# A decoder layer on one core: rules for when side work may be given out, row-tile due times, and the number of gather buffers

## The chip, the cores and the metric

The kernel runs on one core of a Trainium2 chip. The core has a matrix engine (TensorE, "PE" in the profile; its weight loads are listed apart as "PEld"), a vector engine (VectorE, "DVE"), a scalar engine (ScalarE, "ACT"), a general engine (GpSimd, "POOL"), and an engine that only issues transfers here (SyncE, "SP"). Each works through its own instructions in order; they wait for one another by semaphores. Transfers are carried by 16 DMA engines. TensorE writes into PSUM, a small memory of eight banks; everything else lies in SBUF or in the chip's main memory.

The metric is the device time of one execution, in microseconds; the median of the runs counts. A profiled execution gives the trace, which is told in microseconds from the start of its span.

## What is computed

A layer over 4 sequences of 512 tokens, 512 channels each, all in float32:

```python
x = x + attn(layernorm(x), wq, wk, wv, wo)      # 32 heads, 8 kv heads, width 64, rope, causal
x = x + xattn(layernorm(x), ctx)                # both sides rounded to fp8 per block, then a product
x = x + moe(layernorm(x), Wg, W1, W3, W2, sw1, sw3, sw2)

def quant_dequant_act_1x128(x):                 # weights: the same with one scale per 128x128 block
    xb = x.reshape(E, M, K // 128, 128)
    amax = jnp.max(jnp.abs(xb), axis=-1, keepdims=True)
    safe = jnp.maximum(amax, 1e-4)
    q = (xb * (448.0 / safe)).astype(jnp.float8_e4m3fn)
    return (q.astype(jnp.float32) * (safe / 448.0)).reshape(E, M, K)

# moe: each token goes to its best of 8 experts, at most 256 tokens an expert
out = jnp.take(oe, jnp.minimum(flat, E * C - 1), axis=0) * (gate * keep)[:, None]
shared = jax.nn.silu(xt @ sw1) * (xt @ sw3) @ sw2
return out + shared
```

The second term is no attention: each of the 4 sequences is multiplied with its own 512 x 512 context matrix after both were rounded block by block. The third has a shared feed-forward network for every token and eight routed ones.

## The kernel before, in words

The program is straight-line: Python code decides once in which order the instructions of every engine stand. Three stages follow one another.

**Attention with side work.** The scores of one batch are worked in 40 half steps (`SPB`), two to a step. In the loop at the end of the attention part (around L1122), a half step emits: the score matmuls of the next half step (`scores`, whose results VectorE takes to `pm` with the row minimum and ScalarE turns into exponentials), the products with v of finished heads (`weighted`), then fill work (`work.upto`), then the transposes of the probabilities (`turned`: `pt`, copied to `pT` half by ScalarE, half by VectorE, L981 and L987). The fill work is everything else: the projections q, k, v, o of this and the next batch, and the "chain" of the layers between: `CHAIN` at L719 names its jobs.

- `hs`, `h`: layer norm and transposes of the next batch's input (`job_h` L289: four transposes, each copied by ScalarE).
- `cs`, `c`: scales of the context matrix (`job_cs` L474: block maxima, a transpose `pam`, VectorE's `cmx` and `cdg` L493 and L495, a small product `par`) and its rounded, transposed form (`job_c` L503).
- `s`: row statistics after attention. `t`: one job for each of four row tiles (`job_t` L554): scale on GpSimd, round, transpose, four products `py` whose scaled results `y` (VectorE, L592, two buffers) are added to the rows by GpSimd.
- `w`: router, gates, positions, and the scatter of the rows to the experts' places.

A rounding (`quantize_round` L434) is four VectorE instructions on 128x512 elements, L438 to L445.

**The plan.** `Fill` keeps a book: `at` is its own clock, `spent` the TensorE work given out, `gpsimd` (L267 to L269) the moment up to which it believes GpSimd busy, `cool` a moment before which no further chain block is given out. A job is a Python generator. It yields a positive number for TensorE work done, a negative one for a pause in half steps, or a triple: a kind ("dve" or "quiet"), a pause, and how many microseconds of VectorE work come next. Such heavy pieces are given out against the half step's allowance (3.2 at L1122, 4.4 at L1128); a "quiet" one is passed over while `gpsimd` lies ahead of `at`. `first` (L809) picks the next job in order of wanted time, `step` (L827) runs it to its next yield and sets `cool` 0.2 half steps (a half step is `HALF`, 7250 ns) after each chain block, and `upto` (L847) alternates heavy pieces, chain blocks and projections until the half step's share is spent. `need` (L872) forces what the scores cannot wait for. PSUM's banks are shared by tag at L95: four "sp" (scores, `pt`), one "av", three "mm" for all fill work.

The due time of `t` job j is `ze + 2 + j`, counted in half steps (L795); jobs 2 and 3 also wait for jobs 0 and 1, j - 2 each.

**Shared expert and experts.** After the last scores the shared network's units (`shared_up`, `shared_down`) are TensorE's work, with what is left of the chain put in between every few matmuls (`between`, L1247). Then the eight experts run, each with its weights loaded ahead.

**The end.** The last units of the shared network run with rounds of up to four gathers: `gather` (L1328) asks for a row tile `xt` (six buffers, a load on SP's queue) and issues an indirect transfer of the experts' rows to `og` (five buffers, on GpSimd's queue); `combine` (L1338) adds them on VectorE and, where the row is finished, issues its store on SP's queue.

## Time and profile before

| | us |
|---|---|
| median of 3 runs | 1621.65 (1620.45 to 1622.72) |
| the profiled execution, its own time | 1620.97 |
| its span, from first to last instruction | 1619.2 |
| TensorE busy | 1569.1 |
| VectorE busy | 821.8 |
| ScalarE busy | 513.1 |
| GpSimd busy | 332.4 |
| mean granted TensorE clock | 0.989 of full |

How to read the profile's lines. A waits line names the engine, line and tile that waited, what ended the wait, and then total, number and longest. A timeline line gives start, length, engine, line, operation, tiles (written <- read), shapes and count; in brackets the engine's idle time before it and who ended that. A line of stretches gives the stretch, its length, each engine's busy time with its instructions, then the granted TensorE clock (PEclk), the busy share of the DMA engines, and GB/s. Ends of matmuls are modelled.

By stage, TensorE's busy time:

| stretch, us | length | PE busy | DVE busy | ACT busy | POOL busy |
|---|---|---|---|---|---|
| 0 to 80 | 80 | 76.10 | 35.44 | 29.45 | 13.11 |
| 80 to 440 | 360 | 351.29 | 224.44 | 152.75 | 80.03 |
| 440 to 800 | 360 | 340.31 | 235.26 | 146.27 | 103.19 |
| 800 to 1160 | 360 | 351.33 | 209.97 | 138.42 | 91.93 |
| 1160 to 1260 | 100 | 100.00 | 52.27 | 7.61 | 24.22 |
| 1260 to 1619 | 359 | 350.04 | 64.42 | 38.66 | 19.92 |

Attention with its side work ends a little before 1160; the shared network with the last batch's chain follows to about 1260, then the experts and the end.

### The profile page before, as it was taken

To read this page: it belongs to the slowest core of one execution; us is meant where nothing else is said; L and a number is where in the kernel's file an instruction comes from. 1 tells how busy PE (TensorE), PEld (TensorE's weight loads), DVE (VectorE), ACT (ScalarE), POOL (GpSimd) and SP (SyncE) were. 2 spreads that over 40 slices of the span, in tenths; PEclk is the share of its full clock that TensorE was granted. 3 is DMA by queue.
4 is the path that set the end of the run, shared out by engine and by line. 5 is a ranking of instruction groups with operands and counts; after the bars stand their busy time and mean duration, and the time that the engine had idled before them with its cause. 6 is when DMAs were issued, how large, how long until landed. Compare 5 with 4: busy or idle time off the path is not lost.

```text
span 1619.2 us, 19846 instructions
## 1 busy us (share of the span) xinstructions
PE 1569.1 (97%) x6664; PEld 861.4 (53%) x6664; DVE 821.8 (51%) x2399; ACT 513.1 (32%) x1539; POOL 332.4 (21%) x293
## 2 busy tenths in 40 slices
PE   9999999998999999998999999989999999999997
PEld 5555555554545545454555545455444557767653
DVE  4466644578865446885654587683355211111113
ACT  2445343443425343443434345351000101101100
POOL 2031220213342121325212033420232000000012
PEclk9999999999999999999999999999999999999999
DMA  4483441623435243443415251355141253556327
GB/s 137 119 241 98 94 129 46 163 78 87 106 90 138 69 120 112 98 99 91 133 48 159 73 135 36 93 167 177 45 170 39 65 201 131 169 165 234 133 84 254
DMA packets 118918, 195.32 MB, mean 121 GB/s; under 512 B 17184, under 2 KB 36640, under 8 KB 118304
## 3 DMA queue, kind: packets, MB, share of 16 engines
q10 hardware_dynamic: 65760, 101.46, 22.5%
q1 hardware_dynamic: 50496, 84.20, 16.9%
q0 software_dynamic: 2560, 8.39, 1.6%
q8 instruction: 53, 0.87, 0.2%
q14 instruction: 49, 0.40, 0.1%
HBM read 136.07 MB, written 28.57 MB: 102 GB/s over the span
## 4 chain that ended last, share of the span: by engine, by line
PE 82%; DVE 8%; DMA 4%; issue 1%; POOL 1%; ACT 1%; SPq 1%; ACTq 0%; DVEq 0%; POOLq 0%
PE py L397 14%; PE psq L303 11%; PE p_e L1162 9%; PE p_s L1162 9%; PE sc L920 8%; PE av L1001 7%; PE pt L970 6%; PE epy L1190 4%; PE psv L345 4%; PE ys L1190 3%; PE psk L303 3%; DVE pm L943 2%; DMA tsq<-t2q 1%; DMA xt<-x 1%; PE ptr_h L252 1%
## 5 line engine op out<-in xcount | busy, mean ns | idle before, releaser
L953 ACT ACTIVATE pm<-pm,mn 128x256 f32<-128x256 f32 (+3 forms) x512 | 281.0, 550 | 383.1 <-DVE mn L943 358.2
L943 DVE CUSTOM_DVE_ANT_0 pm<-sc,mask 128x256 f32<-128x256 f32 (+3 forms) x512 | 216.6, 486 | 100.3 <-PE sc L920 98.1
L303 PE MATMUL psq<-hT,wq 128*128 128x512 f32 x512 | 242.2, 609 | 7.7 <-DVE cmx L493 7.4
L397 PE MATMUL py<-wo,aT 128*128 128x512 f32 x512 | 242.1, 608 | 5.2 <-DVE y L592 4.8
L920 PE MATMUL sc<-kT,t1q 64*128 64x384 f32 (+3 forms) x1024 | 170.9, 450 | 12.4 <-DVE pT L987 7.5
L987 DVE COPY pT<-pt 128x128 f32<-128x128 f32 (+3 forms) x256 | 113.8, 484 | 118.3 <-PE pt L970 105.1
L268 POOL TENSOR_TENSOR t1q<-t1q,tsq 128x512 f32<-128x512 f32 x64 | 82.2, 1286 | 433.5 <-DMA tsq<-t2q 320.8
L970 PEld LDWEIGHTS pt<-ident,pm 128*128 128x128 f32 x1280 | 146.8, 142 | 36.0 <-issue 31.0
L970 PE MATMUL pt<-ident,pm 128*128 128x128 f32 x1280 | 155.6, 276 | 0.7 <-ACT pm L953 0.7
L1162 PE MATMUL p_s<-h3x,slot_s 128*128 128x512 f32 x352 | 155.6, 594 | 0.0
L1162 PE MATMUL p_e<-xT,slot_e 128*128 128x256 f32 x704 | 155.1, 380 | 0.0
L981 ACT COPY pT<-pt 128x128 f32<-128x128 f32 (+3 forms) x256 | 97.5, 431 | 180.3 <-PE pt L970 145.0
L303 PEld LDWEIGHTS psq<-hT,wq 128*128 128x128 f32 x512 | 93.7, 194 | 111.0 <-issue 101.1
L1001 PE MATMUL av<-pT,v 128*64 128x512 f32 (+3 forms) x1024 | 152.1, 439 | 0.0
L397 PEld LDWEIGHTS py<-wo,aT 128*128 128x128 f32 x512 | 93.9, 193 | 109.1 <-issue 90.2
L1162 PEld LDWEIGHTS p_e<-xT,slot_e 128*128 128x128 f32 x704 | 132.6, 190 | 23.2 <-issue 5.8
L920 PEld LDWEIGHTS sc<-kT,t1q 64*128 64x128 f32 x1024 | 87.4, 187 | 97.5 <-issue 69.7
L1001 PEld LDWEIGHTS av<-pT,v 128*64 128x64 f32 x1024 | 68.6, 136 | 106.0 <-issue 96.1
L1162 PEld LDWEIGHTS p_s<-h3x,slot_s 128*128 128x128 f32 x352 | 65.8, 190 | 77.7 <-issue 75.6
L268 POOL TENSOR_TENSOR acc<-acc,y 128x512 f32<-128x512 f32 x64 | 80.6, 1269 | 96.4 <-DVE y L592 95.0
L953 ACT ACTIVATION_READ_ACCUMULATOR pm<-pm,mn 128x1 f32 x512 | 95.5, 186 | 0.0
L268 POOL TENSOR_TENSOR aT<-aT,rrb 128x512 f32<-128x512 f32 x64 | 81.4, 1296 | 55.6 <-DMA rrb<-rrd 41.9
(174 smaller groups left out, 1349.3 us busy)
## 6 DMA issues: line engine op xcount, KB each, us to landing
slot_e<-in_L_ffn_W_dram SPq DMA_DIRECT2D x14, 1280.0 KB, 12.6
wq<-in_L_attn_wq_dram ACTq DMA_DIRECT2D x16, 1024.0 KB, 5.8
tsq<-t2q SPq DMA_DIRECT2D x256, 64.0 KB, 2.3
wo<-in_L_attn_wo_dram ACTq DMA_DIRECT2D x16, 1024.0 KB, 5.8
rrb<-rrd ACTq DMA_DIRECT2D x32, 512.0 KB, 7.2
slot_e<-in_L_ffn_W_dram SPq DMA_DIRECT2D x7, 1408.0 KB, 6.6
kT<-t1k ACTq DMA_DIRECT2D x64, 128.0 KB, 2.9
xt<-x SPq DMA_DIRECT2D x28, 256.0 KB, 5.7
```

The source lines that it names most:

```text
L268: nc.gpsimd.tensor_tensor(*args)
L303: nc.tensor.matmul(ps, w[:, k, c0 : c0 + P], hTs[b][:, k, :], start=(k == 0), stop=(k == KC - 1),)
L397: nc.tensor.matmul(py, aT[:, r, j * P : (j + 1) * P], wts["o", a][:, r, :], start=(r == 0), stop=(r == 3),)
L920: nc.tensor.matmul(scs[g][:, o : o + nk], qTs[b, p][g * HD : (g + 1) * HD, it * P : nk], kTs[b, p // 2][g * HD : (g + 1) * HD, 0:nk], star ...
L943: nc.vector.tensor_tensor_reduce(out=pm[:, o : o + nk], in0=scs[g][:, o : o + nk], in1=mask[:, T - nk : T], scale=-(HD**-0.5), scalar=3.0e ...
L953: nc.scalar.activation(pm[:, o : o + nk], pm[:, o : o + nk], AF.Exp, bias=mn, scale=-1.0, accum_out=rss[b, a][:, col : col + 1],)
L970: nc.tensor.transpose(pt[:, j * P : (j + 1) * P], pms[g][:, j * P : (j + 1) * P], ident)
L981: nc.scalar.copy(pT[:, 0 : it + 1, it * P : nk], pt[:, o : o + nk].rearrange("p (j t) -> p j t", t=P),)
L987: nc.vector.tensor_copy(pT[:, it + 1, 0:nk], pt[:, o : o + nk])
L1001: nc.tensor.matmul(av[g * HD : (g + 1) * HD, j * P : T], vs[b][:, j, v0 : v0 + HD], rhs, start=(j == 0), stop=(j == TB - 1),)
L1162: nc.tensor.matmul(pp[:, 0:cols], w13[:, k, o : o + P], xT[:, k, 0:cols], start=(k == 0), stop=(k == KC - 1),)
L1190: nc.tensor.matmul(py, gT[:, c, (t + i) * P : (t + i + 1) * P], w2[:, c, :], start=(c == 0), stop=False,)
```

## The change

Four edits to the plan and one number in the end part.

- The roundings in `job_c` and `job_t` yield "quiet" in place of "dve". In `job_cs` the piece of VectorE work on `pam` (`cmx`, `cdg`) becomes a heavy "quiet" piece of 0.7 with no pause, after the transpose's yield of 110; the product `par` follows after a "quiet" pause of 0.6 (before: a pause of 1) with 1.0 of VectorE work.
- `first` no longer exempts a chain job's first step from `cool`. `upto` takes a new value `busy` and moves `cool` to at least `at + busy`: 1900 in the first half step of a step, 900 in the second, 0 elsewhere. Where `upto` finds nothing to give out while `cool` lies ahead, it sets `cool` to now and looks once more.
- The due times of the row tiles are `ze + 2 + f * j` with f = 2, 3, 3, 1 for batches 0 to 3.
- `og` has eight buffers in place of five.

```diff
@@ job_cs
         nc.tensor.transpose(pt[0:n, 0:P], am.rearrange("p i k -> p (i k)"), ident)
+        yield 110
+        yield "quiet", 0, 0.7
         mx = const.tile([n, 1], F32, tag="cmx", name=f"cmx_{b}")
         nc.vector.tensor_reduce(mx, pt[0:n, 0:P], AX.X, ALU.max)
         dg = const.tile([n, n], F32, tag="cdg", name=f"cdg_{b}")
         nc.vector.tensor_scalar_mul(dg, ident[0:n, 0:n], mx)
-        yield 110
-        yield -1
+        yield "quiet", 0.6, 1.0
         pr = bank("mm", f"par_{b}")
@@ job_c
-                yield "dve", 0.6, 2.4
+                yield "quiet", 0.6, 2.4
                 load_c(nt + 2)
                 qs.append(quantize_round(vs[nt], f"c{b}_{nt}"))
@@ job_t
         v = quantize_scale(h, inv, f"x{b}_{j}")
-        yield "dve", 1 * pace(b), 2.4
+        yield "quiet", 1 * pace(b), 2.4
         q = quantize_round(v, f"x{b}_{j}")
@@ the list of jobs
-                ze + 2 + j, 8 * 220, ("t", b, j), job_t(b, j),
+                ze + 2 + (1, 3, 3, 2)[B - 1 - b] * j, 8 * 220, ("t", b, j), job_t(b, j),
@@ first
-                    if not room and job.ready and self.at < self.cool:
+                    if not room and self.at < self.cool:
                         continue
@@ upto
-        def upto(self, n, pace, room=0.0):
+        def upto(self, n, pace, room=0.0, busy=0):
+
+            self.cool = max(self.cool, self.at + busy)
             while True:
...
                             if self.spent == spent:
-                                return
+                                if self.cool <= self.at:
+                                    return
+                                self.cool = self.at
                             continue
@@ the loop over half steps
-        work.upto(n, goal, 3.2)
+        work.upto(n, goal, 3.2, 1900)
...
-        work.upto(n + 1, goal, 4.4)
+        work.upto(n + 1, goal, 4.4, 900)
@@ gather
-        ogs[i] = ep.tile([P, D], F32, tag="og", bufs=5, name=f"og_{i}")
+        ogs[i] = ep.tile([P, D], F32, tag="og", bufs=8, name=f"og_{i}")
```

## The prediction

> **What bounds the kernel now.** I read the page's busy shares first, then the list of who TensorE waited for, then the timeline at the longest of those waits, then stretches with the granted clock, and last the end of the run.

> ```profile
> PE 1569.1 (97%) x6664; PEld 861.4 (53%) x6664; DVE 821.8 (51%) x2399; ACT 513.1 (32%) x1539; POOL 332.4 (21%) x293
> ```

> TensorE is the bound: 1619.2 - 1569.1 = 50.1 us are not covered by matmuls, and the change alters no matmul. So all it can win is idle time of TensorE, and what idle time drags behind it. The waits (in total, times, longest):

> ```profile
> PE sc L920 <- DVE pT L987: 7.5, 8, 3.0
> PE psq L303 <- DVE cmx L493: 7.4, 2, 4.8
> PE ptr_h L252 <- ACT cT L520: 5.0, 2, 2.5
> PE py L397 <- DVE y L592: 4.8, 3, 2.1
> PE py L590 <- DVE y L592: 3.9, 5, 1.7
> PE sc L920 <- issue: 3.2, 2, 2.8
> ```

> These six are 31.8 us in 22 waits: few and long. VectorE's and GpSimd's timelines at the longest one (TensorE idle from 374.69 to 379.48):

> ```profile
> 372.71 0.08 DVE L943 DVE_READ_ACCUMULATOR2_ANT mn<- 128x1 f32 x1
> 373.19 1.30 DVE L438 TENSOR_SCALAR qm_x<-qv_x 128x512 int32<-128x512 int32 x1
> 374.53 1.37 DVE L442 TENSOR_SCALAR qm_x<-qm_x 128x512 f32<-128x512 f32 x1
> 375.93 1.63 DVE L443 TENSOR_TENSOR qv_x<-qv_x,qm_x 128x512 f32<-128x512 f32 x1
> 377.60 1.64 DVE L445 TENSOR_TENSOR qq_x<-qv_x,qm_x 128x512 bf16<-128x512 f32 x1
> 379.16 0.27 DVE L493 TENSOR_REDUCE cmx<-pam 16x1 f32<-16x128 f32 x1
> ```

> ```profile
> 372.93 1.28 POOL L268 TENSOR_TENSOR t1k<-t1k,tsk 128x512 f32<-128x512 f32 x1 [10.56 <-PE ptr_h L252]
> 374.16 4.53 POOL L268 TENSOR_TENSOR aT<-aT,rrb 128x512 f32<-128x512 f32 x3
> ```

> The four instructions of a rounding have medians of 0.42, 0.43, 0.69 and 0.69 us (the tile's view), 2.2 us; here, beside GpSimd, they take 5.9 us, and `cmx`, which frees the PSUM bank that the next q projection takes, stands behind them. Then the clock, in stretches just after such waits (PEclk, the granted clock, is the third value from the right):

> ```profile
> 380.00:382.80 2.80, 2.80 (x4) 1.00 (x3) 2.80 (x7) 0.00 (x0) 1.58 (x2) 0.50 0.10 23
> 495.50:498.90 3.40, 3.35 (x17) 3.28 (x17) 0.48 (x3) 2.28 (x6) 1.04 (x1) 0.50 0.02 3
> 666.20:669.50 3.30, 3.30 (x4) 1.48 (x5) 3.30 (x7) 1.20 (x4) 3.30 (x4) 0.50 0.81 180
> 737.90:744.60 6.70, 5.61 (x7) 2.35 (x8) 4.50 (x9) 1.19 (x4) 5.27 (x6) 0.50 0.48 137
> ```

> Seven such stretches, 29.7 us in sum as I cut them, run at half clock; each 3.4 us of it loses 1.7 us, about 15 us in all. A stall is thus dearer than its idle time.

> [...] 0.42 becomes 1.30 us and 0.69 becomes 1.63. [...] here waits of 4.8 and 2.6 us were followed by it, one of the two 2.5 us ones was and the other not, so shorter gaps count with luck. [...]

> **Part 1, roundings and `cmx` wait for a quiet GpSimd.** No instruction is added. "quiet" looks at the plan's book of GpSimd work, not at GpSimd. Followed through the code of the kernel before, that book is busy at only three of 32 roundings: the second row tile of batches 0, 1 and (barely) 2; the first two are the waits at 374.69 (4.8 us) and 663.62 (2.5 us). At 374.69 the rounding will be given out some three q blocks later. But VectorE was at its score minima until 373.19 anyhow and GpSimd was late against the book (10.56 us idle before `t1k`), so the overlap may stay: the gain lies between nothing and 4.8 + 1.7 (clock) = 6.5 us; I take 3. At 663.62 the row tile also moves (part 3): between 0 and 2.5 + 1.7 = 4.2; I take 3. `cmx` fits the same half step's allowance (3.2 - 2.4 = 0.8, it asks 0.7), so it still follows the rounding; its bank is held no longer. Queued behind a later rounding are the DVE halves of the `pT` copies; were these late, `sc` would wait (the 7.5 us row).

> **Part 2, chain blocks held back.** At the start of a half step ScalarE has its exponentials: its timeline at 489.90 to 493.39 is full of them, and the copies of `ptr_c` and `ptr_h` stand behind, so TensorE waits 2.5 us at 491.99 and again at 780.92. There the h transposes were given out although the cooling time ran, because a job's first step was exempt. Now they come after 1.9 us of other work, in whole blocks of 0.86: two or three projection blocks, about 2 us of cover. I take 1.5 of each 2.5, and the clock at 495.5 (1.7): 4.7 us, between 0 and 2 x 2.5 + 1.7 = 6.7. What is late next: the held blocks come nearer to the `pt` transposes, and their copies (0.57 us each; four in a row 2.06 us at 783.92) stand before ScalarE's `pT` copies. No trace shows this; I put it at 4 us for the whole run (two new waits of about 1 us, like those at 352.33 and 423.47, and one stretch of half clock), between 0 and 25.

> **Part 3, row tiles spread.** Due times bind only where nothing else does. Row tiles 2 and 3 wait for tiles 0 and 1 anyhow, and in batches 0 and 2 tile 1 falls into the same half step as before; batch 3's factor is 1, so nothing moves. What moves is batch 1: tile 1 by two or three half steps, tile 3 after it. At 734.88 and 736.92 TensorE waits 1.67 and 2.07 us for `y`, whose buffers GpSimd frees after three `aT` products of 3.72 us; then 6.7 us at half clock. Tile 3's share should leave. I take 2 us, between -3 (a new meeting with the next `aT` products) and 1.67 + 2.07 + 3.4 = 7.1. The twin at 447.70 and 449.18 stays.

> **Part 4, gather tiles 5 to 8.** The last four combines wait for `xt`, not for `og`:

> ```profile
>   DMA xt<-x: 15.6, 6
> DMA to landing us min/median/max: 2.8/6.4/7.5
> ```

> (the `xt` tile's view, 1560 to the end: what held the combines, and its loads.) Each round of four `xt` loads is queued on SP behind the previous round's output stores. More `og` tiles let the gathers run one round ahead[...]. TensorE ends at 1610.04, VectorE's last two additions start at 1614.41: at most 4.4 us to win; I take 2, down to 0 if landing doesn't shorten.

> **The sum.** -3 - 3 - 4.7 + 4 - 2 - 2 = -10.7 us. In batch 3's row and router work between the shared expert's matmuls and in the experts TensorE shows no wait (100.00 us busy in 1160 to 1260), so nothing there. The profiled run took 1620.97 us for its span of 1619.2; 1621.0 - 10.7 = 1610.3. The median of the runs is 0.7 us above the profiled one, so 1611.0.

> **Rivals.**
> - Weak: the book is too far from the chip, the waits at 374.69 and 663.62 stay, and only part 2 and the end count: 1621.6 - 4.7 - 2 + 4 = about 1619. For it: the 10.56 us lateness. Against: the twin waits at 491.99 and 780.92, 288.9 us apart, show the plan's order recurring faithfully.
> - Full: every wait aimed at goes, 6.5 + 4.2 + 6.7 + 7.1 + 4.4 = 28.9 without new ones: 1593.
> - Slower: held blocks collide with the `pT` copies. The rule holds back about 12 blocks a batch (four row-tile transposes, the router's four or five, `h`, two of `job_cs`), 36 in the three batches worked beside attention; if two in five make `sc` wait 1.1 us (15 x 1.1 = 16.5) and every third of these halves the clock (5 x 1.7 = 8.5), it costs 25 instead of 4: 1611 + 21 = 1632. It decides from about 15 us of new stalls on. For it: `sc` behind `pT` is already the largest row. Against: ScalarE is busy 32%, and its row of that wait is only 0.9 us.

> **Chances.** 0.2% is 3.2 us, about what a measurement of this kernel tells from no change. Likeliest case (1604 to 1617) 0.50; weak (1615 to 1623) 0.20, of which 0.09 is faster by more than 3.2 us and 0.11 within; full 0.08; slower 0.22, of it 0.01 within. Faster 0.67, same 0.12, slower 0.21. The range 1597 to 1625 leaves out about 0.17 of the slower case and 0.03 of the full one.

> **What would show it.** Right: no `psq` wait on `cmx` above 2 us, no `ptr_h` wait on `cT` above 1.5 us, roundings near 2.3 us, fewer half-clock stretches than seven, `y` waits at 447 to 450 still there, gathers no longer waiting for `xt` L1339, end about 7 us behind the last matmul. Wrong: PE busy time changed; `sc` waiting more on ScalarE's `pT`; new half-clock stretches.

## The result, and the profile after

| | before | after |
|---|---|---|
| median of 22 runs each, us | 1622.75 (1618.12 to 1627.81) | 1617.43 (1612.92 to 1625.05) |
| ratio, 95% interval | | 0.9965 [0.9953, 0.9977] |
| span of the profiled execution, us | 1619.2 | 1617.6 |
| TensorE idle ahead of its last matmul, us | 39.5 | 39.6 |
| last matmul to the end, us | 9.2 | 7.7 |
| half clock from 14 us to the last rounds, us | 30.7 in 7 stretches | 34.1 in 7 |
| 32 roundings, in sum, us | 85.6 | 98.4 |

The last four rows are added up from the records of the trace: gaps between matmuls, the end of the last one, the granted clock, and each rounding from the start of L438 to the end of L445. The change made the kernel faster by 0.35%, 5.7 us by the ratio and 5.3 by the medians, about half of the 10.7 forecast. The slowest and the fastest of the 22 executions of one kernel lie 10 to 12 us apart, so a single pair of profiles, here 1.6 us apart in span, cannot carry a gain of 5.7; the timed runs do, and the profiles show what changed place.

Most of that spread goes with the granted clock, which is on record for each execution of the kernel after and of all later runs. In 50 executions of the kernel before (those beside the runs with one part left out) it lies between 0.984 and 0.991, and 0.001 more goes with 1.6 us less. Its mean is 0.9875 there and 0.9890 in the 22 executions of the kernel after. By this, as an estimate, some 2 us of the 5.7 are clock, although the one pair of profiles shows more half clock after than before.

The busy shares of the kernel after (engine, busy time, share, instructions):

```profile
PE 1568.9 (97%) x6659; PEld 858.7 (53%) x6664; DVE 838.9 (52%) x2399; ACT 518.1 (32%) x1541; POOL 336.3 (21%) x293
```

TensorE is as busy as before, and VectorE is busy for 17 us more with the same instructions; the roundings' sum has grown by 12.8. That is not what roundings kept apart from GpSimd should look like. Whom TensorE waited for after the change (in total, times, longest):

```profile
PE sc L925 <- DVE pT L992: 5.5, 7, 2.7
PE ptr_h L252 <- ACT cT L521: 4.7, 2, 2.4
PE sc L925 <- DVE mn L948: 3.9, 4, 2.5
PE ptr_h L252 <- DVE t1q L314: 2.8, 2, 1.6
PE ptr_h L252 <- DVE qq_x L445: 2.5, 1, 2.5
PE ptr_h L252 <- DVE h L246: 2.3, 1, 2.3
...
PE prr L363 <- DVE rr L360: 2.0, 1, 2.0
```

Both waits on `cmx` (7.4 us) are gone, and most of those on `y`. In their place stand waits on `mn`, `t1q`, `qq_x`, `rr`. The two on `cT`, which part 2 aimed at, are 4.7 us instead of 5.0; they only lie later, at 513 and 807 instead of 492 and 781. The first rounding of batch 0's row tiles in the kernel after, on VectorE and then GpSimd (start, duration):

```profile
372.87 0.42 DVE L438 TENSOR_SCALAR qm_x<-qv_x 128x512 int32<-128x512 int32 x1
373.32 1.50 DVE L442 TENSOR_SCALAR qm_x<-qm_x 128x512 f32<-128x512 f32 x1
374.86 1.65 DVE L443 TENSOR_TENSOR qv_x<-qv_x,qm_x 128x512 f32<-128x512 f32 x1
376.54 1.64 DVE L445 TENSOR_TENSOR qq_x<-qv_x,qm_x 128x512 bf16<-128x512 f32 x1
```

```profile
373.27 1.27 POOL L268 TENSOR_TENSOR t1k<-t1k,tsk 128x512 f32<-128x512 f32 x1 [9.94 <-DMA tsq<-t2q]
374.50 4.82 POOL L268 TENSOR_TENSOR aT<-aT,rrb 128x512 f32<-128x512 f32 x3
```

It is tile 0's rounding and no longer tile 1's, and it meets the same GpSimd work. GpSimd had been idle for 9.94 us until a transfer landed and then worked off what had queued up. Another row tile's rounding began at 730.38 and met four `aT` products; there TensorE waited for the rounding itself (last field: idle time before the instruction, and what ended it):

```profile
736.50 0.40 PE L252 MATMUL ptr_h<-ident_b,qq_x 128*128 128x128 bf16 x4 [2.50 <-DVE qq_x L445]
```

Ten of the 32 roundings took over 3 us, where before there were seven.

### The profile page after: what moved, and what is told of

Read it like the earlier page. It is cut to its first block, busy times and chain, and to the rows that moved or that the text cites. A ratio compares the mean times of both kernels' runs of the same rounds, so it can differ in the third digit from the quotient of the medians.

```text
span 1617.6 us, 19823 instructions
## 1 busy us (share of the span) xinstructions
PE 1568.9 (97%) x6659; PEld 858.7 (53%) x6664; DVE 838.9 (52%) x2399; ACT 518.1 (32%) x1541; POOL 336.3 (21%) x293
## 5 line engine op out<-in xcount | busy, mean ns | idle before, releaser
L397 PE MATMUL py<-wo,aT 128*128 128x512 f32 x512 | 243.9, 610 | 3.2 <-POOL aT L268 1.7
L303 PE MATMUL psq<-hT,wq 128*128 128x512 f32 x512 | 236.6, 598 | 2.2 <-DVE y L593 1.7
L925 PE MATMUL sc<-kT,t1q 64*128 64x384 f32 (+3 forms) x1024 | 173.8, 455 | 12.8 <-DVE pT L992 5.5
L268 POOL TENSOR_TENSOR t1q<-t1q,tsq 128x512 f32<-128x512 f32 x64 | 83.5, 1305 | 437.5 <-DMA tsq<-t2q 243.6
L1006 PE MATMUL av<-pT,v 128*64 128x512 f32 (+3 forms) x1024 | 156.6, 448 | 0.0
L303 PEld LDWEIGHTS psq<-hT,wq 128*128 128x128 f32 x512 | 91.7, 190 | 100.8 <-issue 95.8
L397 PEld LDWEIGHTS py<-wo,aT 128*128 128x128 f32 x512 | 92.5, 192 | 96.0 <-issue 84.7
L268 POOL TENSOR_TENSOR acc<-acc,y 128x512 f32<-128x512 f32 x64 | 81.5, 1279 | 180.0 <-DVE y L593 179.0
L268 POOL TENSOR_TENSOR aT<-aT,rrb 128x512 f32<-128x512 f32 x64 | 82.7, 1318 | 26.0 <-DMA rrb<-rrd 26.0
```

Of the source, the lines that this page charges most:

```text
L268: nc.gpsimd.tensor_tensor(*args)
L303: nc.tensor.matmul(ps, w[:, k, c0 : c0 + P], hTs[b][:, k, :], start=(k == 0), stop=(k == KC - 1),)
L397: nc.tensor.matmul(py, aT[:, r, j * P : (j + 1) * P], wts["o", a][:, r, :], start=(r == 0), stop=(r == 3),)
L925: nc.tensor.matmul(scs[g][:, o : o + nk], qTs[b, p][g * HD : (g + 1) * HD, it * P : nk], kTs[b, p // 2][g * HD : (g + 1) * HD, 0:nk], star ...
L1006: nc.tensor.matmul(av[g * HD : (g + 1) * HD, j * P : T], vs[b][:, j, v0 : v0 + HD], rhs, start=(j == 0), stop=(j == TB - 1),)
```

## The experiments

All ratios are to the kernel before, run beside the kernel in question. Parts are numbered as in the prediction.

**Each part alone.** The edits are those of the diff: part 1 the three "quiet" changes, part 2 `first`, `upto` and its two calls, part 3 the due time, part 4 the `og` buffers.

Part 1:

> Before with part 1 alone (roundings and the cmx piece quiet). Theory M (stalls move): the plan's book of GpSimd runs ahead of the chip, so the held roundings meet GpSimd's late work; the 32 roundings take no less than the 85.6 us of before, TensorE's idle time before the end stays within 3 us of 39.5, time within 3 us of before. Theory S (the sum of the prediction): the two waits on cmx (7.4 us) go, idle time falls by 4 us or more, time falls by 4 to 8 us.

Part 2:

> Before with part 2 alone (no exemption of first steps, busy 1900 and 900, the second look). Theory M: the two ptr_h waits of 2.5 us on cT at 492 and 781 turn up elsewhere, idle time within 3 us of 39.5, time within 3 us. Theory S: they shrink to about 1 us each, new sc waits of about 2 us come, time within 2 us of before. Rival (slower): sc waits on pT grow from 8 us to over 20, time over 10 us longer.

Part 3:

> Before with part 3 alone (row tiles' due times). Theory S: only batch 1 changes; the wait for y at 735 to 737 shrinks, 2 us faster (between 3 slower and 7 faster). Theory M: row tiles of batch 1 move and meet other work, time within 3 us. Batches 0, 2 and 3 look as before in both.

Part 4:

> Before with part 4 alone (eight og tiles). Both theories: the gathers of a round are issued before its xt loads, the stretch from the last matmul to the end falls from 9.2 to about 7.5 us, nothing else changes; 1 to 3 us faster. If the time is 4 us or more faster, something besides the end has changed.

| part alone | ratio, interval | us | the prediction's term |
|---|---|---|---|
| 1 | 1.0002 [0.9992, 1.0012] | +0.3 | -6 |
| 2 | 1.0102 [1.0086, 1.0119] | +16.6 | -0.7 |
| 3 | 0.9963 [0.9950, 0.9975] | -6.0 | -2 |
| 4 | 0.9983 [0.9973, 0.9993] | -2.8 | -2 |

Alone they add up to +8, together they are -5.7: the parts of this plan are not additive. In part 1's run the `cmx` waits went, but two waits of `py` that the profile gives no releaser for (7.5 us) came, and `sc` behind `pT` grew from 7.5 to 11.5 us; the roundings took 85.2 us in sum. Part 2 came out slower, as its rival said, but not by `sc` behind `pT` (7.1 us, where before there were 7.5). TensorE's idle time grew from 39.5 to 51.1 us, and the largest new wait is 6.9 us at 1133.83, for a rounding of the context matrix. ScalarE's timeline before it:

```profile
1134.47 1.30 ACTq L376 DMA_DIRECT2D rrb<-rrd  x2
1135.80 1.28 ACT L1177 ACT_TABLE_LOAD   x1 [7.02 <-DMA h3d<-h3T]
1137.09 0.60 ACT L1177 ACTIVATE gT<-p_s 128x512 f32<-128x512 f32 x1
```

ScalarE did no work for 7 us, five of them ahead of its own issue of a load (ACTq) from `rrd`, which an earlier transfer fills; the shared expert's activation and behind it VectorE, idle for 15 us, followed late. That held-back blocks had put this issue in a worse place of ScalarE's queue is argued, not shown. The other 10 us of part 2's price I did not trace one by one.

**One part left out, and two together.**

Without part 1:

> The changed kernel without part 1 (parts 2, 3 and 4). Theory A (parts add): 1.0102 x 0.9963 x 0.9983 = 1.005 of before, so about 14 us slower than the changed kernel. Theory I (part 1 matters only together with part 2, which pushes roundings to where GpSimd is busy): as slow as A or slower, with the 32 roundings above 98 us and a wait of some us after 1110. Theory N (part 3 alone rescues part 2): at 0.9965, like the changed kernel.

Without part 2:

> The changed kernel without part 2 (parts 1, 3 and 4). If part 2 costs time here as it does alone: 0.995 of before, some 3 us faster than the changed kernel; the chain of batch 2 ends as early as in before. If part 2 pays in the changed kernel: slower than 0.9965.

Without part 3:

> The changed kernel without part 3 (parts 1, 2 and 4). Theory A: 1.0002 x 1.0102 x 0.9983 = 1.009, 14 us slower than before. Theory I: part 1 heals part 2, so within 0.998 to 1.000, and part 3 gives the rest.

Parts 3 and 4 only:

> Before with parts 3 and 4 alone. The two touch different stages, so they add: 0.9963 x 0.9983 = 0.9946, about 9 us faster than before and 3 us faster than the changed kernel. No wait on cmx, a tail of about 7.5 us.

| kernel | ratio, interval |
|---|---|
| parts 2, 3, 4 | 0.9989 [0.9972, 1.0005] |
| parts 1, 3, 4 | 0.9955 [0.9941, 0.9969] |
| parts 1, 2, 4 | 0.9987 [0.9977, 0.9997] |
| parts 3, 4 | 0.9956 [0.9939, 0.9974] |
| all four (the kernel after) | 0.9965 [0.9953, 0.9977] |

Parts 3 and 4 give all of the gain. Adding parts 1 and 2 to them changes nothing that can be told (0.9956 and 0.9965). Beside part 2, part 1 seems to be worth 0.24% (0.9989 without it, though the intervals just overlap); without part 2, nothing. And part 2's price of 1.0% is paid only where it stands alone: with part 1 beside it (parts 1, 2, 4) or with part 3 (parts 2, 3, 4) it is gone for the most part, and so is the wait of 6.9 us. Why either of the two is enough stays open.

**Why part 3 wins: `cmx`.** In part 3's run `cmx` at 364.48 follows a rounding of 2.2 us, and both `psq` waits are gone. Is that the cause, or the spread of the row tiles? Two trials change only when the context scales' job goes on to `cmx`. First ahead:

```diff
@@ job_cs, after the block maxima @@
-        yield -1
+        yield -0.1
```

> The kernel before with one number changed: after its block maxima the context scales' job waits 0.1 of a half step instead of 1, so in batches 0 and 1 the transpose into pam and the cmx reduction are given out ahead of row tile 0's and 1's roundings and no longer right behind the one that meets GpSimd. The row tiles keep their order and due times. Theory A (part 3 won because it took cmx away from behind the slow rounding): both psq waits on cmx (7.4 us with the half clock after them) go and the time falls like part 3's, by 4 to 7 us, ratio 0.9957 to 0.9975, though the rounding itself stays near 5.9 us. Rival B (part 3 won by the later row tiles, fewer meetings on VectorE): ratio 0.999 to 1.001. Rival C (waits only change place): cmx waits go, others of the same 7 us come, ratio within 0.001 of 1.

It came out at 1.0034 [1.0022, 1.0045]. The `cmx` waits went, and the `pam` transpose, now too early, waited 6.2 us in two places for the block maxima; in batch 2, whose jobs moved too, the scores waited 5.1 us behind `aT`. It does not tell. Then behind, by one half step (`yield -2`). In the plan this leaves every row tile's rounding in its half step; the transposes of tile 1 in batches 0 and 1 and the context copies of batch 0 do move by one, other than the expectation says:

> The kernel before with one number changed: after its block maxima the context scales' job waits 2 half steps instead of 1, so that cmx is given out one half step later and not right behind the rounding that meets GpSimd; every row tile, context copy and router job stays in its half step. Theory A (part 3 won because cmx no longer stood behind the slow rounding): both psq waits on cmx go and no new one above 1.5 us comes in their place, ratio 0.9955 to 0.9975. Rival B (part 3 won by the row tiles' spread): cmx waits go but the ratio is 0.999 to 1.001, since other waits take their place as in the trial with cmx ahead.

Result: 0.9965 [0.9953, 0.9978], part 3's gain with no row tile's rounding moved. Waits in that run:

```profile
PE py L397 <- DVE y L592: 4.8, 3, 2.1
PE sc L920 <- issue: 3.1, 2, 2.7
PE pam L491 <- DVE t1q L314: 3.1, 1, 3.1
PE py L397 <- POOL t1q L268: 2.5, 1, 2.5
```

The `psq` row on `cmx` is gone. Two new waits of 3.1 and 2.5 us stand in their place, behind the same slow roundings (6.1 us each); the condition "no new one above 1.5 us" failed. The timed runs speak for `cmx` and against the spread of the row tiles, but they do not settle it: the `cmx` waits went in five trials, and two of them gained about 6 us (part 3 alone and this one) while three gained nothing (part 1 alone, part 2 alone, and `cmx` ahead, slower by 0.34%). That a small reduction which frees a PSUM bank leaves its place behind a contended rounding was not enough by itself; it counts what comes in its place. By the profile one cannot say which microseconds were saved.

**Why part 1 does not keep roundings quiet.** For each of the ten slow roundings of the kernel after I compared the trace with the plan's book at the moment it was given out. In all ten the book already showed GpSimd idle, in nine for less than 2.0 us and in one for 4.8 (the expectation below counted nine and six). So the rule passed them, and the chip's GpSimd was behind the book. A margin holds them longer:

```diff
@@ first @@
-                    and not (job.quiet and self.gpsimd > self.at)
+                    and not (job.quiet and self.gpsimd + (3000 if n < 165 else 0) > self.at)
```

> The kernel after with a margin on the book of GpSimd's work: up to the last attention half step, a job that wants GpSimd quiet is held until the book has been idle for 3 us, not merely idle. In the kernel after, every rounding that took over 3 us was given out while the book was idle, six of the nine for less than 2.0 us. Theory (the book runs ahead of the chip by a few us, so held roundings still meet GpSimd's work): the 32 roundings fall from 98.4 us in sum to 75 to 85 us. As to time: if contended roundings cause what is left of the waits, 3 to 6 us less than the kernel after, ratio to before 0.993 to 0.995; if a rounding's length hardly matters once cmx does not stand behind it, ratio as the kernel after, 0.996 to 0.998; and slower, 0.998 to 1.005, if the later chain costs more than the contention. Rival (the meetings are with GpSimd work given out after the rounding): the sum stays above 92 us.

0.9910 [0.9888, 0.9932], and the roundings fell to 82.9 us. TensorE idled for 29.2 us instead of 39.6 and ran its last matmul at 1591.9 instead of 1609.9. But from there to the end it took 15.6 us: the chain ended one half step later, used up one unit of the shared expert earlier, and a round of four outputs was left over behind the last matmul. So the time beat every range that the expectation gave for it, in spite of a worse end. With the margin only up to half step 150 the plan's end stays as it was. On all four parts, then on part 1 alone, on parts 1, 3 and 4, and on parts 1 and 2:

> The kernel after with the 3 us margin up to half step 150 and nothing else. Theory (part 2 pays once roundings are quiet, the margin pays once chain blocks are spaced): ratio to before 0.987 to 0.990, 0.002 above the run with the mended end and at least 0.004 under the run without part 2 (0.9944). Rival (the mended end carried more than its 3 us of tail, parts 2 and the margin do not help each other): ratio 0.9925 to 0.9955.

> Part 1 alone with the same margin. Theory (part 1 alone brought 0 because the book is idle while GpSimd still works): roundings 76 to 84 us in sum instead of 85.2, the y and cmx waits gone, ratio 0.990 to 0.996. Rival (part 1 needs parts 2 and 3 to have room for the held roundings): ratio 0.998 to 1.002, with as much idle time of TensorE as part 1 alone had (38 us).

> Parts 1, 3 and 4 with the same margin up to half step 150, without part 2 and with the end as in the kernel after. Theory (part 2 only moves the waits for ScalarE's copies; what counts is that roundings are quiet): ratio 0.985 to 0.990, about 3 us above the run with the mended end. Rival (the margin needs part 2's spacing, since the held jobs bunch up without it): ratio 0.991 to 0.996, with ptr_h waits on cT of 5 us in two places as in the kernel before.

> Parts 1 and 2 with the margin, without parts 3 and 4. Part 1 with the margin alone gave 0.9994. Theory (same as for the run beside it): the ptr_c waits on ScalarE's h3T copies (5.5 us) go, ratio 0.990 to 0.995. Rival (part 3 is what the margin needs): 0.9975 to 1.002.

| | without part 2 | with part 2 |
|---|---|---|
| part 1, no margin | 1.0002 | not run (with part 4 too: 0.9987) |
| part 1, margin | 0.9994 [0.9983, 1.0005] | 0.9894 [0.9874, 0.9913] |
| parts 1, 3, 4, no margin | 0.9955 [0.9941, 0.9969] | 0.9965 [0.9953, 0.9977] |
| parts 1, 3, 4, margin | 0.9944 [0.9930, 0.9959] | 0.9880 [0.9854, 0.9905] |

On parts 1, 3 and 4 either alone brings next to nothing, and on part 1 the margin alone too; together margin and part 2 bring 0.8 to 1.1%. I had expected the margin to be enough, and part 2 to be a cost whatever stood beside it; both were wrong. What part 2 adds can be seen in part in the run of part 1 with the margin, where the roundings' sum is about the same (84.0 us; 83.6 with all four parts and the margin). TensorE around 514, and ScalarE:

```profile
513.50 1.42 PE L252 MATMUL ptr_h<-ident,h 128*128 128x128 f32 x8
514.76 1.02 PE L345 MATMUL psv<-wv,hT 128*128 128x512 f32 x2
518.85 0.59 PE L252 MATMUL ptr_c<-ident_b,qq_c 128*128 128x128 bf16 x4 [3.07 <-ACT h3T L630]
```

```profile
514.85 0.72 ACT L954 ACTIVATE pm<-pm,mn 128x512 f32<-128x512 f32 x1 [8.17 <-DVE mn L944]
...
518.24 0.56 ACT L630 COPY h3T<-ptr_h 128x512 f32<-128x512 f32 x1
```

Two groups of transposes were given out straight after the scores. Their copies stood behind the row of exponentials from 514.85 to 518.24, and TensorE waited 3.07 us, until the first of them had ended. This is the wait that part 2 is meant to prevent. In the run of all four parts with the margin (0.9880), the waits are these:

```profile
PE sc L925 <- DVE pT L992: 8.1, 9, 3.0
PE ptr_h L252 <- ACT hT L294: 4.0, 3, 1.4
PE ptr_h L252 <- ACT cT L521: 3.0, 2, 1.5
```

No wait on `h3T`, and those on `cT` down from 2.4 us each in the kernel after to 1.5. It is not this wait alone: with parts 1 and 2 and the margin those on `h3T` (5.5 us without part 2) are gone, but so are most of those of `py` on `aT` (6.2 us, now 0.6), which I did not trace. The `qm_x` tile's view shows the row tiles' roundings in the kernel after, and then in this run (count, shortest/median/longest in ns, first and last start):

```profile
L438 DVE TENSOR_SCALAR qm_x<-qv_x x16: 407/420/1311, 372.9 to 1223.5; 128x512 int32<-128x512 int32 x16
L445 DVE TENSOR_TENSOR qq_x<-qv_x,qm_x x16: 691/691/1643, 376.5 to 1225.1; 128x512 bf16<-128x512 f32 x16
```

```profile
L438 DVE TENSOR_SCALAR qm_x<-qv_x x16: 407/420/454, 388.3 to 1213.8; 128x512 int32<-128x512 int32 x16
L445 DVE TENSOR_TENSOR qq_x<-qv_x,qm_x x16: 691/692/1415, 389.9 to 1215.4; 128x512 bf16<-128x512 f32 x16
```

The medians are the same; what is left of the contention is in the longest. The first row tile's rounding now starts 15 us later. That the gain comes from quieter roundings is not shown: their sum, 83.6 us, is hardly below the 85.6 of the kernel before, six of the 32 still take over 3 us where before there were seven, and the margin moves everything behind a held rounding. That the new order is the cause, and not the quiet, stands untested. Why part 2 does nothing while roundings are still slow is only argued too: a slow rounding delays `mn` and so the exponentials, and the 1.9 us of cover run out before ScalarE has begun its row (in the kernel after the exponentials of that half step began at 511.78, a copy from `ptr_c` stood at 515.17 behind them).

**The end, and `cT` on VectorE.** VectorE's additions at the end of the kernel after:

```profile
1609.61 2.17 DVE L1344 SCALAR_TENSOR_TENSOR xt<-og,gk,xt 128x512 f32<-128x512 f32 x3 [2.06 <-DMA xt<-x]
1612.18 0.75 DVE L1344 SCALAR_TENSOR_TENSOR xt<-og,gk,xt 128x512 f32<-128x512 f32 x1 [0.40 <-DMA xt<-x]
1612.85 1.28 DVE L1236 TENSOR_TENSOR xt<-ys,xt 128x512 f32<-128x512 f32 x2
```

The last matmul had ended at 1609.9; the combines of the last round still waited for their `xt` loads, issued behind the previous round's stores. The next kernel issues a round's gathers and loads one round ahead, on top of parts 3 and 4, and takes the experts' idle input tiles for every second round:

```diff
-        for i, last in fresh:
-            gather(i)
         if units:
             f, *args = units.pop(0)
             f(*args)
+        then = give(odd)
         for i, last in fresh:
             combine(i, last)
+        fresh = then
```

> Parts 3 and 4 with the end of the kernel changed: the gathers and the loads of the x rows of a round are given out ahead of the previous round's combines instead of behind them, with four more tiles for the rows (the experts' input tiles, free by then). Theory (after part 4 what is left of the tail is the xt loads, queued on SP behind the previous round's output stores and then waited for by the combines): from the last matmul to the end 7.8 us become 4.5 to 5.5, and the time is 2 to 3.5 us under that of parts 3 and 4 alone, ratio to before 0.9935 to 0.9945. Rival (the landing of the output stores sets the end, or the loads now collide with the gathers): tail over 7 us, ratio 0.9950 to 0.9960.

And with `ptr_c`'s copies on VectorE:

```diff
-            nc.scalar.copy(
+            nc.vector.tensor_copy(
                 cT[:, :, nt * P : (nt + 1) * P], transpose4(qs[nt], f"ptr_c_{b}_{nt}")
```

> As the last one, and in addition the four copies per batch of ptr_c into cT are on VectorE instead of ScalarE. Theory (the 2.5 us waits of ptr_h on ScalarE's cT copy are ScalarE's queue of exponentials, which part 2 only met later): both ptr_h waits on cT go and with them up to 1.7 us of half clock each: 3 to 7 us less than the run without it, ratio about 0.990 to 0.992. Rival (the copies delay the score minima and pT copies on VectorE, or the wait goes over to the rr copy, which stands in the same queue): ratio as without it or above, 0.9935 to 0.997, with new sc waits.

The first is at 0.9940 [0.9916, 0.9963], with 4.7 us from the last matmul to the end instead of 7.8; its interval overlaps that of parts 3 and 4, so it is the trace that shows the shorter end. The second is not faster, 0.9960 [0.9949, 0.9970]: the waits on `cT` went over to the `rr` copy in the same queue of ScalarE (4.3 us in two places). This fits a queue that is late as a whole, not one copy.

**The best version:** all four parts, the margin up to half step 150, and the end issued ahead.

> The kernel after with the 3 us margin on the book of GpSimd's work up to half step 150 (so that the last stage has its units as in the kernel after) and with the gathers and x loads of the end given out ahead of the previous round's combines. In the run with the margin TensorE's last matmul ended 18 us earlier than in the kernel after, but a lone round at the end made the rest 15.6 us instead of 7.7. Theory (that gain is the quiet roundings' and stays when the end is mended): tail 4.5 to 5.5 us, TensorE's idle time before the end 28 to 32 us, ratio to before 0.984 to 0.989. Rival (the gain came with the changed last stage, or from one lucky profile): ratio 0.990 to 0.9935.

0.9866 [0.9847, 0.9885], 1602.37 us. TensorE idles for 31.4 us ahead of its last matmul, and the end takes 4.7. The mean clock of its five executions is 0.9936 (before: 0.9878 beside it), so by the 1.6 us for each 0.001, an estimate, some 9 of its 22 us are clock. Its last combines and additions on VectorE:

```profile
1588.61 1.41 DVE L1348 SCALAR_TENSOR_TENSOR xl<-og,gk,xl 128x512 f32<-128x512 f32 x2
1595.92 1.29 DVE L1236 TENSOR_TENSOR xt<-ys,xt 128x512 f32<-128x512 f32 x2 [5.90 <-PE ys L1205]
```

The combines are done 6 us ahead; the additions wait for TensorE alone.

## Why the prediction was right or wrong, point by point

- **Bound and sign:** right. No matmul changed, TensorE's busy time is the same, and the gain is of the kind predicted.
- **Part 1, -6:** this step failed. The prediction said that "quiet" looks at the book and not at GpSimd, and that "the overlap may stay"; then it took the middle of its bounds, -3 twice. What the runs show in its place: the roundings still met GpSimd. With part 1 alone the rounding of 373.19 began at 376.71 and took 5.2 us instead of 6.1, because GpSimd, idle for 10.7 us until a transfer landed, was late by more than the book knew; all 32 took 85.2 us instead of 85.6, and 98.4 in the kernel after. Alone the part is worth +0.3 us, the end of its bounds. The term also counted only what left: the wait behind `cmx` went, and other waits came.
- **Part 2, -4.7 and +4:** failed on the gain. "Two or three projection blocks, about 2 us of cover" did not remove the waits on `cT`: 4.7 us of 5.0 stayed, at a later place. The cost was bounded at 0 to 25 and put at 4; alone the part costs 16.6. Within the whole it is +1.6 us (0.9965 against 0.9955), not to be told from nothing. The collision named there, held blocks ahead of the `pT` copies, did not come: `sc` behind ScalarE's `pT` does not grow (0.9 us before, none in part 2's run).
- **Part 3, -2:** right in sign, wrong in mechanism, and too small (-6.0 alone). "In batches 0 and 2 tile 1 falls into the same half step as before" treated the due time as a gate only. It also sets a job's rank and the share of work given to each half step; in the plan `h` of batch 1 moves by two half steps, and the context scales' job beside batch 0's row tiles finishes two half steps earlier. So `cmx` left the slow rounding, which the prediction had booked under part 1. Of the waits on `y` that the term aimed at, the one of 1.7 us at 735 left, but in sum they are 8.8 us in part 3's run against 8.7.
- **Part 4, -2:** right: -2.8 alone, with 7.2 us instead of 9.2 from the last matmul to the end. The `xt` loads landed in a median of 4.8 us instead of 6.4; what shortened them no run shows. That the combines wait for `xt` and not `og` was right too; issuing the loads ahead took another 3 us.
- **Clock:** the price of 1.7 us holds, 3.41 us at a granted clock of 0.50. As it says, the waits of 4.8 and 2.6 us and one of the two of 2.5 were followed by half clock; what it calls luck went with where the wait lay (last section).
- **The sum:** with 1's term at nothing and 3's at -6, and 2 at nothing within the whole, it would have been -8; the measured -5.7 shows again that the terms do not add.
- **Rivals:** "weak" had the right reason, a book too far from the chip, and 1619 for the time. It thought part 2 would still pay. The slower one happened to part 2 alone (1.0102) by another mechanism and was gone in the whole.

## What to carry to other kernels

A rule that keeps two engines apart by a plan's own book works only as well as the book follows the chip: count in the trace how many of the protected instructions still collide, and try a margin on the book. Try the parts of a schedule change in pairs too, since a part that costs 1% alone was worth 0.6% here beside the margin. A changed due time may move everything that is ranked by it, so compare the whole order of instructions and not only the job concerned.

## What the runs showed of the hardware that was not expected

Beside GpSimd's instructions, small operations of VectorE lost about as much time as large ones. In the kernel after, one of the row statistics' products on 128x4 elements took 1.17 us instead of 0.16 while GpSimd worked on `t1q`:

```profile
630.35 0.16 DVE L240 TENSOR_TENSOR r0b<-veb,rsb 128x4 f32<-128x4 f32 x1
630.55 1.17 DVE L241 TENSOR_TENSOR r0b<-r0b,rsb 128x4 f32<-128x4 f32 x1
631.95 0.16 DVE L240 TENSOR_TENSOR r0b<-veb,rsb 128x4 f32<-128x4 f32 x1
```

```profile
630.44 1.27 POOL L268 TENSOR_TENSOR t1q<-t1q,tsq 128x512 f32<-128x512 f32 x1 [4.46 <-DVE veb L238]
```

It ends at 631.72, just behind the one GpSimd instruction (631.71). In that trace 11 operations that read and write 128x4 elements took over 0.5 us (0.63 to 1.24), and each ended 0.02 to 0.03 us behind an instruction of GpSimd. The large ones lost about as much each (0.43 to 1.50 us, 0.69 to 1.65 us), so the small ones suffered most in proportion.

```profile
492.10:495.50 3.40, 1.01 (x8) 0.86 (x8) 3.30 (x6) 3.00 (x9) 1.26 (x1) 1.00 0.36 91
778.80:782.20 3.40, 2.12 (x21) 1.28 (x17) 3.33 (x14) 3.36 (x11) 0.84 (x2) 1.00 0.35 80
782.20:785.60 3.40, 2.14 (x18) 1.90 (x19) 2.18 (x2) 3.00 (x9) 1.98 (x2) 1.00 0.31 84
785.60:789.00 3.40, 3.38 (x27) 2.76 (x26) 2.69 (x6) 2.43 (x6) 0.00 (x0) 1.00 0.02 5
```

So 2.0 us of idle time in one window of 3.41 us were followed by half clock in all 78 cases here, and of the twin waits of 2.5 us only the one that lay in a single window was. That this place differs from one execution to the next fits the spread of clocks, but one trace of each kernel cannot show it. The half clock of a single profile says little. Part 1's profile (47.8 us of it) had a clock of 0.983 where its 14 executions reach from 0.982 to 0.989, and the profile of the trial with `cmx` ahead (20.5 us) one of 0.991, the highest of its 20. The mean over the executions tells more, and single waits of 2 us and more are what to remove here: between 20 us and the last matmul there are eight in the trace before, five after, and one in the best version, with mean clocks of 0.9875, 0.9890 and 0.9936.
